# Two mixer layers with routed experts: other places for the gated pieces, the router's loads and the last norms

## The chip, the cores and the metric

The kernel runs on one core of a Trainium2 chip. The time is the device time of one execution in microseconds (us), the median of several runs. A separately profiled execution gives the trace. PE is the matmul engine (PEld its weight loads), DVE the vector engine, ACT the activation engine, POOL the general-purpose engine, SP the queue that only issues transfers. Each engine carries out its instructions in the order of the program.

## The reference

There are 16 sequences of 256 tokens, 128 wide, 4096 tokens in all. Each of two layers computes

```
xn = layernorm(x)
x  = x + mixer(xn) * silu(experts(xn))
```

- Layer 0 mixer: gated linear attention with 4 heads, keys of 128 and values of 32. `q`, `k`, `v`, a gate `g` and a decay `gk = log_sigmoid(xn Wgk1 Wgk2 + b) / 16` are projections. Within chunks the decayed product of `q` and `k` is masked to the lower triangle and weighs `v`, and a state carries over chunks; the result is normed per head, multiplied by `silu(g)` and projected by `Wo`.
- Layer 0 experts: softmax over 8 gates, the best two per token. An expert is `a * sigmoid(b)` with `a, b = split(xn W1[e] + b1[e])`, 256 each, then the common `Wo` and `bo`; the two are summed by weight.
- Layer 1 mixer: causal softmax attention with 16 heads of 8.
- Layer 1 experts: 16 experts, the best two, `tanh(xn mag) * cos(softplus(xn freq) + 0.1 + phase)` over 256 columns, then `down`; the weighted sum of the two is normed (RMS, weight `norm_w`).

## The kernel before

The tokens are eight blocks of 512 (`NB`), each four tiles of 128 (`NTL`). `xs` (the stream), `xnx` (normed, with two routing weights per token) and `xnTs` (normed, turned) stay on the chip. The mixer's result of a block is written over `xnTs` (`s_sbs`). Experts work on slots: each (token, choice) pair gets a place sorted by expert, 128 slots of one expert are a tile, 71 tiles in layer 0 and 79 in layer 1. The rows of a tile are fetched by an indirect DMA on POOL's queue (`slot_in`, line 378), and results are scattered back by another (`slot_out`, line 390).

The order on PE, DVE, ACT and SP is the order in which Python writes the instructions. Generators write them in pieces; each `yield` is a break at which another generator may write a piece.

- **Start.** `normed0` norms the eight blocks (`normed_T`, line 207: statistics and normalisation on DVE, turning on PE) and `route` (line 246) sorts the slots; at every second break `main` writes a piece. `main` is `gated()`: for each block `decays` (11 pieces: logarithms, running sums, scaled `q` and `k`) alternates with `mixed` of the block before (13 pieces: masked products `pA` copied by line 609, `v` weighed, norm, projection).
- **Layer-0 products.** `experts0` (line 677) goes over the tiles in 18 batches of `CP0 = 4`. Per tile: eight PE matmuls into one of two `pf` buffers (line 728), the sigmoid on ACT (lines 733 to 737), the gate on DVE (line 744, written one tile later). Per batch: the second product `pe` (line 758) and its weighing (lines 760 to 762). Its weights `wt0` come by SP into six buffers, with a small bias tile each. Every break calls `spread()`, which issues one waiting row fetch or result, and adds `1.0 / RATE` = 1.25 to what is due of `main`; each whole one due writes a gated piece and calls `spread()` again. Fetches and results stand behind the last instruction marked `passed`.
- **The passage.** `for _ in main: next(cstream)`: after each remaining gated piece, one round of `combined`. A round advances every live block by one stage, and starts one more block if its mixer is done. Stages of a block: fetch the two results (`gg`); sum, sigmoid; update of the stream and statistics; normalisation and turning; router scores (line 784).
- **Early layer 1.** What is left of `combined` runs with three pieces of attention per round (`fill(3)`), then `route` with one per break. Attention's pieces are `both` (scores in two forms, lines 928 and 961, whose maxima on DVE and exponentials on ACT follow), `queries`, `weighted` (line 1011, copied to `yt` by line 1016), `normed`, `turned`, `projected`, and five of `setup` per block (`qT` copied by line 889).
- **Layer-1 products.** After `route`, weights and rows of the first batch of `CPB = 8` tiles are asked for. `experts` (line 1108) has its own breaks, each with a piece of attention.
- **The tail.** The rest of attention, three pieces at a time, alternates with rounds of `finished` (line 1188): fetch of the results, sum, RMS norm, sigmoid, multiplication by the mixer's `s_sbs`, sum with the stream, output. A block enters when attention is done with it.

Of the kernel before, what the change touches and what calls it, by code (L numbers as in the profile page):

```python
# [10 lines left out]
F32 = mybir.dt.float32  # L11
# [28 lines left out]
RATE = 0.8  # L40
# [18 lines left out]
def two_layer_kernel(  # L59
# [147 lines left out]
    def normed_T(pool, ps, b):  # L207

        xb, xn = xs[b], xns[b]
        mv = pool.tile([P, NTL, 2], F32, tag="mv", name="mv", bufs=3)  # L210
        for t in range(NTL):
            st = pool.tile([P, 6], F32, tag="st", name="st", bufs=2)
            nc.vector.bn_stats(st, xb[:, t, :])
            nc.vector.bn_aggr(mv[:, t, :], st)
        rs = pool.tile([P, NTL], F32, tag="rs", name="rs", bufs=3)
        nc.scalar.activation(rs, mv[:, :, 1], AF.Ln, bias=eps5)
        nc.scalar.activation(rs, rs, AF.Exp, scale=-0.5)
        yield
        pt = ps[0].tile([P, NTL, P], F32, tag=ps[1], name="ptn")
        for t in range(NTL):  # L220
            nc.vector.tensor_scalar(  # L221
                xn[:, t, :], xb[:, t, :], mv[:, t, 0:1], rs[:, t : t + 1], ALU.subtract, ALU.mult
            )
            nc.tensor.transpose(pt[:, t, :], xn[:, t, :], ident)  # L224
        nc.scalar.copy(xnTs[b], pt.rearrange("p t k -> p (t k)"))
        yield
# [19 lines left out]
    def route(pool, ps, sc, ne, slt, lay, emap, rm, ptag, tkw):  # L246
# [87 lines left out]
        yield  # L334
# [3 lines left out]
        for c in range(2):  # L338
            for n0 in range(0, NT32, NH):
# [16 lines left out]
                yield  # L356

# [6 lines left out]
        yield  # L364
        tb = pool.tile([P, 2, slt], F32, tag="rt_tb", name="tb")
        nc.scalar.copy(tb, pT)
        row, tok = tb[:, 0, :], tb[:, 1, :]
        nc.vector.scalar_tensor_tensor(row, row, float(P), tok, ALU.mult, ALU.add)
        nc.vector.tensor_scalar(seconds[lay], row, 4096.0, None, ALU.is_ge)
        nc.vector.scalar_tensor_tensor(toks[lay], seconds[lay], -4096.0, row, ALU.mult, ALU.add)  # L370
# [106 lines left out]
    c_ps = []  # L477
    ccmb = ctx.enter_context(ExitStack())
    ET = mybir.EngineType
    with ExitStack() as cg:  # L480
# [118 lines left out]
        def mixed(b):  # L599
# [3 lines left out]
            for s in range(NSQ):  # L603
                for t in (2 * s, 2 * s + 1):
                    pA = ps.tile([P, GH, P], F32, tag="ps", name="pA")
                    for h in range(GH):
                        ts = slice(t * P, (t + 1) * P)
                        nc.tensor.matmul(pA[:, h, :], kk[:, h, ts], qg[:, h, ts], start=True, stop=True)  # L608
                    passed(nc.vector.copy_predicated(
                        a_bufs[t % 2], bc(upper.bitcast(I32).unsqueeze(1), [P, GH, P]), pA  # L610
                    ))
                    yield
                pf = ps.tile([P, GH, P], F32, tag="ps", name="pf0")
                for h in range(GH):
                    ts = slice((2 * s + 1) * P, (2 * s + 2) * P)
                    nc.tensor.matmul(pf[:, h, :], kg[:, h, s, :], qg[:, h, ts], start=True, stop=True)
                a_off = wk_.tile([P, GH, P], F32, tag="aoff", name="aoff")
# [59 lines left out]
        def experts0(hp, pe_):  # L677
# [3 lines left out]
            def loads(j0, n):  # L681
                wts, nbs = [], []
                for j in range(j0, j0 + n):
                    reg = tile_expert(emap0, j, E0)
                    wt = hp.tile([P, 2 * H0], F32, tag="wt0", name="wt0", bufs=6)
                    nc.sync.dma_start(wt, w1[:, bass.ds(reg, 1), :].rearrange("p e h -> p (e h)"))
                    nb = hp.tile([P, 4], F32, tag="nb0", name="nb0", bufs=8)
# [24 lines left out]
            for k, (j0, n) in enumerate(batches):  # L712
# [8 lines left out]
                for i in range(n):  # L721
# [5 lines left out]
                    for c in range(4):  # L727
                        nc.tensor.matmul(  # L728
                            pf[:, c, :], wts[i][:, c * P : (c + 1) * P], xgT[:, i, :], start=True, stop=True
                        )  # L730
                    sg = hp.tile([P, 2, P], F32, tag="sg0", name="sg0", bufs=3)
# [24 lines left out]
                for i in range(n):  # L756
                    for c in range(2):
                        nc.tensor.matmul(pe[:, i, :], gts[i][:, c, :], sb_wo0[:, c, :], start=(c == 0), stop=(c == 1))  # L758
                og = hp.tile([P, CP0, D], F32, tag="og0", name="og0")
# [7 lines left out]
        def combined(b):  # L767
# [13 lines left out]
            yield from normed_T(cmb, c_ps, b)  # L781
# [10 lines left out]
        with tc.manual_schedule(engines={ET.Activation, ET.PE, ET.DVE, ET.SP}):  # L792
# [25 lines left out]
            hp0.close()  # L818
            cmb = ccmb.enter_context(tc.tile_pool(name="cmb", bufs=2, side="left"))
            sc1 = cmb.tile([P, NT32, E1], F32, name="sc1", bufs=1)  # L820
            with tc.tile_pool(name="gpc", bufs=2, space=PSUM) as pc_:
                c_ps[:] = [pc_, "pc"]
                cstream = staged([combined(b) for b in range(NB)], lambda b: b in mixed_)
                for _ in main:
                    next(cstream, None)
# [4 lines left out]
    with ExitStack() as c1:  # L830
# [41 lines left out]
        def attention():  # L872
# [5 lines left out]
            def setup(b):  # L878
# [6 lines left out]
                def q_part(i):  # L885
# [3 lines left out]
                    passed(nc.vector.tensor_copy(qT[i], pq))  # L889
# [111 lines left out]
            def weighted(i):  # L1001
# [14 lines left out]
                later.append(lambda: passed(nc.vector.tensor_copy(yt, yx)))  # L1016
# [75 lines left out]
        def weights_of(j0, n):  # L1092

            wts = []
            for j in range(j0, j0 + n):
                reg = tile_expert(emap1, j, E1)
                wt = hp.tile([P, WROW], F32, tag="wt", name="wt", bufs=CPB + 1)
# [4 lines left out]
        def rows_of(j0, n):  # L1102

            xg = hp.tile([P, n, DX], F32, tag="xg", name="xg")
# [83 lines left out]
        def finished(b):  # L1188

            gg = results(hp, 1, b, "xg")  # L1190
# [17 lines left out]
            nc.vector.tensor_tensor(acc, acc, s_sbs[b], ALU.mult)  # L1208
            yield
            nc.vector.tensor_tensor(sq, sq, acc, ALU.mult)  # L1210
            nc.vector.tensor_tensor(sq, xs[b], sq, ALU.add)
            nc.sync.dma_start(ov[b], sq)
            yield

        wk_ = c1.enter_context(tc.tile_pool(name="l1wk", bufs=2, side="right"))
        pS = c1.enter_context(tc.tile_pool(name="l1pS", bufs=2, space=PSUM))
        ps = c1.enter_context(tc.tile_pool(name="l1ps", bufs=2, space=PSUM))
        pf_ = c1.enter_context(tc.tile_pool(name="l1pf", bufs=2, space=PSUM))
        pieces, ahead, later, done = attention(), [], [], set()
# [21 lines left out]
        with tc.manual_schedule(engines={ET.Activation, ET.PE, ET.DVE, ET.SP}):  # L1241
# [3 lines left out]
            for _ in cstream:  # L1245
                fill(3)
            with tc.tile_pool(name="rt1", bufs=1) as rt1:
                for _ in route(rt1, pf_, sc1, E1, SLT, 1, emap1, starts(rt1, E1), "pf", {"tag": "pf"}):
                    fill(1)
            ccmb.close()  # L1250
            hp = c1.enter_context(tc.tile_pool(name="l1h", bufs=2))
            batches = [(j0, min(CPB, SLT - j0)) for j0 in range(0, SLT, CPB)]
            got = weights_of(*batches[0]), rows_of(*batches[0])
# [10 lines left out]
            ends = staged([finished(b) for b in range(NB)], lambda b: b in done)  # L1264
            while fill(3):
                next(ends, None)
            for _ in ends:
                pass
# [53 lines left out]
```

## Time and profile before

| | before |
|---|---|
| runs, median (lowest to highest) | 1162.42 us (1159.44 to 1168.86), 3 runs |
| profiled execution | 1160.43 us, span 1158.7 us |
| busy in the span | PE 878.0 (76%), DVE 763.6 (66%), ACT 588.5 (51%), POOL 394.3 (34%) |
| mean granted PE clock | 0.863 |
| layer-0 products, 115 to 420 us | PE busy 252.07 |
| passage, 425 to 531 us | PE busy 62.67, DVE 61.75 |
| early layer 1, 531 to 643 us | DVE busy 90.40 |
| hand-over, 643 to 660 us | PE busy 8.52 |
| layer-1 products, 660 to 1054 us | PE busy 341.13 |
| tail, 1054 to 1158.7 us | PE busy 68.45 |

The profiled time is that of the whole execution; the span runs from its first to its last instruction. Busy times are sums over an engine's instructions, and a matmul's includes the granted clock: the same matmul takes longer at a lower clock.

### The profile page before, as it was taken

Reading aid. Unit: us, or ns where it says so; the run is one execution under the profiler, and the core shown is the slowest. Engines: PE = TensorE matmul, PEld = TensorE weight load, DVE = VectorE, ACT = ScalarE, POOL = GpSimd, SP = SyncE. Lnnn points to the kernel's source line nnn. Section 1 sums busy time; section 2 is a strip of 40 time slices with the busy share of each in tenths; the row PEclk is TensorE's granted clock in tenths of the full one; section 3 lists DMA queues with packets and bytes.
Section 4 is the critical chain, followed back from the end, with each engine's and each line's share of the span. In section 5 each row is a group of like instructions: output and inputs, shape, how many; then the busy total and the mean of one; then the engine's idle time right before and its main releaser. Section 6 shows DMA issues by size and latency. Waiting matters only on the chain.

```text
span 1158.7 us, 17715 instructions
## 1 busy us (share of the span) xinstructions
PE 878.0 (76%) x6394; PEld 623.3 (54%) x6394; DVE 763.6 (66%) x1442; ACT 588.5 (51%) x1059; POOL 394.3 (34%) x422
## 2 busy tenths in 40 slices
PE   6554887888879854867666688887789899788782
PEld 4323666666657633543334366665576666565451
DVE  5777555665565748544689388767678777785843
ACT  3314576866666735432113265656465666565543
POOL 2000545463535320000111426534554664433110
PEclk9977899998889985677679699999899899998666
DMA  4040497532323222000040413431442243212311
GB/s 121 1 74 11 127 227 152 132 109 79 110 78 91 69 71 73 19 1 1 0 74 1 151 44 112 138 128 29 136 139 77 89 144 128 59 63 71 92 37 36
DMA packets 88415, 95.41 MB, mean 82 GB/s; under 512 B 22228, under 2 KB 64040, under 8 KB 88328
## 3 DMA queue, kind: packets, MB, share of 16 engines
q1 hardware_dynamic: 78632, 74.32, 23.4%
q0 software_dynamic: 9696, 19.97, 6.7%
q8 instruction: 50, 0.82, 0.3%
q14 instruction: 37, 0.30, 0.1%
HBM read 78.03 MB, written 22.51 MB: 87 GB/s over the span
## 4 chain that ended last, share of the span: by engine, by line
PE 43%; DVE 29%; ACT 14%; issue 7%; DMA 4%; POOL 1%; SPq 1%; DVEq 0%; POOLq 0%; ACTq 0%
PE pq L547 5%; PE pf L728 4%; PE Sq L928 3%; PE pe L1178 3%; PE pm L1153 3%; PE pe L758 3%; DVE negm L940 2%; PE Sk L961 2%; DVE vt L1139 2%; PE yx L1011 2%; PE pA L608 2%; DVE vt L1143 2%; DVE z L1135 1%; PE Sq L922 1%; DVE mx L938 1%
## 5 line engine op out<-in xcount | busy, mean ns | idle before, releaser
L390 POOL DMA_INDIRECT yd<-og,row x150 | 157.5, 1050 | 201.1 <-DVE og L762 102.3
L378 POOL DMA_INDIRECT xg<-xnd,tok x150 | 150.9, 1006 | 105.3 <-PE pz L511 52.9
L971 POOL TENSOR_SCALAR_AFFINE_SELECT pr<-pr 128x1024 f32<-128x1024 f32 x64 | 70.8, 1108 | 262.5 <-ACT pr L968 262.3
L968 ACT ACTIVATE pr<-Sk 128x1024 f32<-128x1024 f32 x96 | 98.0, 1021 | 108.0 <-PE Sk L961 107.7
L961 PE MATMUL Sk<-qm,kT 32*128 32x256 f32 x768 | 125.1, 449 | 24.9 <-DVE negm L940 17.3
L928 PE MATMUL Sq<-km,qT 32*128 32x256 f32 x768 | 129.1, 455 | 16.1 <-DVE mx L938 7.8
L728 PE MATMUL pf<-xgT,wt 128*128 128x128 f32 x568 | 84.2, 298 | 28.6 <-issue 12.1
L928 PEld LDWEIGHTS Sq<-km,qT 32*128 32x128 f32 x768 | 70.6, 208 | 63.0 <-issue 34.7
L728 PEld LDWEIGHTS pf<-xgT,wt 128*128 128x128 f32 x568 | 77.4, 209 | 43.4 <-issue 23.5
L961 PEld LDWEIGHTS Sk<-qm,kT 32*128 32x128 f32 x768 | 74.3, 209 | 38.9 <-DVE negm L940 23.2
L940 DVE TENSOR_REDUCE negm<-Sq 128x8 f32<-128x1024 f32 x64 | 78.1, 1220 | 23.5 <-PE Sq L928 14.1
L733 ACT ACTIVATE sg<-pf,nb 128x128 f32<-128x128 f32 x142 | 44.3, 364 | 67.0 <-PE pf L728 66.6
L744 DVE SCALAR_TENSOR_TENSOR gt<-pf,nb,sg 128x128 f32<-128x128 f32 x142 | 42.7, 344 | 40.6 <-ACT sg L737 34.6
L922 PE MATMUL Sq<-mq,identb 128*128 128x512 bf16 x128 | 42.4, 416 | 18.1 <-DVE mx L938 9.5
L1178 PE MATMUL pe<-wt,th 128*128 128x128 f32 x316 | 41.9, 288 | 16.4 <-DVE th L1170 16.3
L1178 PEld LDWEIGHTS pe<-wt,th 128*128 128x128 f32 x316 | 38.8, 199 | 23.9 <-DVE th L1170 12.7
L224 PE MATMUL ptn<-ident,xnx 128*128 128x128 f32 x64 | 18.6, 438 | 41.6 <-DVE xnx L221 41.6
L938 DVE TENSOR_REDUCE mx<-Sq 128x8 f32<-128x1024 f32 x32 | 39.0, 1218 | 15.0 <-PE Sq L928 8.9
L758 PE MATMUL pe<-sb_wo,gt 128*128 128x128 f32 x284 | 41.4, 302 | 8.9 <-DVE gt L744 4.9
L347 ACT ACTIVATE ohj<-hi,place 128x568 bf16<-128x568 bf16 (+1 forms) x16 | 12.8, 798 | 68.2 <-DVE hi L346 65.1
L758 PEld LDWEIGHTS pe<-sb_wo,gt 128*128 128x128 f32 x284 | 38.6, 212 | 15.7 <-DVE gt L744 5.9
L1016 DVE COPY yt<-yx 128x512 f32<-128x512 f32 x32 | 21.9, 686 | 33.8 <-PE yx L1011 33.7
(269 smaller groups left out, 2089.5 us busy)
## 6 DMA issues: line engine op xcount, KB each, us to landing
wt<-bank SPq DMA_DIRECT2D x79, 385.0 KB
wt<-in_w_dram SPq DMA_DIRECT2D x71, 256.0 KB
gg<-yd SPq DMA_DIRECT2D x32, 256.0 KB
xnd<-xnx SPq DMA_DIRECT2D x16, 260.0 KB
xg<-xnd,tok POOLq DMA_INDIRECT x150, 3.1
yd<-og,row POOLq DMA_INDIRECT x150, 2.3
x<-in_x_dram SPq DMA_DIRECT2D x8, 256.0 KB
bank<-in_freq_dram SPq DMA_DIRECT2D x1, 2048.0 KB
```

The costliest lines, as they stand in the source:

```text
L378: return nc.gpsimd.indirect_dma_start(out=xg[:, i, :], out_offset=None, in_=xnds[lay], in_offset=bass.IndirectOffsetOnAxis(ap=toks[lay][:, ...
L390: give = nc.gpsimd.indirect_dma_start(out=yds[lay], out_offset=bass.IndirectOffsetOnAxis(ap=rows[lay][:, j : j + 1], axis=0), in_=og[:, i, ...
L547: nc.tensor.matmul(pq[:, c], w_[:, h * DK : (h + 1) * DK], xnT, start=True, stop=True)
L728: nc.tensor.matmul(pf[:, c, :], wts[i][:, c * P : (c + 1) * P], xgT[:, i, :], start=True, stop=True)
L758: nc.tensor.matmul(pe[:, i, :], gts[i][:, c, :], sb_wo0[:, c, :], start=(c == 0), stop=(c == 1))
L922: nc.tensor.matmul(S[:, c], identb, mq, start=True, stop=False, skip_group_check=True)
L928: nc.tensor.matmul(S[:, c, js, :], qT[part][r, tq], km[r, js, tk], start=not diag, stop=True, skip_group_check=True,)
L940: passed(nc.vector.tensor_reduce(ng, S, AX.X, ALU.max, negate=True))
L961: nc.tensor.matmul(S[:, c, js, :], kT[part][r, tk], qm[r, js, :], start=True, stop=True, skip_group_check=True,)
L968: nc.scalar.activation(pr, S, AF.Exp, scale=scale)
L971: pooled(nc.gpsimd.affine_select(pr_, pr_, pattern=[[0, 8], [1, P]], compare_op=ALU.is_ge, fill=0.0, base=0, channel_multiplier=-1,))
L1178: nc.tensor.matmul(pe[:, i - i0, :], ths[i // 2][:, 2 * (i % 2) + c, :], wts[i][:, 2 * H1 + c * D : 2 * H1 + (c + 1) * D], start=(c == 0), ...
```

## The change

1. In `experts0` a break (`yield`) is added between the product `pf` and its sigmoid, and between `pe` and its weighing. `RATE` goes from 0.8 to 1.33, since there are now 11 breaks per batch of four instead of 6.
2. In `mixed` the break after `pA` stands ahead of the masked copy instead of behind it, and a break is added between `pf0` and its copy: 15 pieces instead of 13.
3. `wt0` has eight buffers instead of six, `nb0` nine instead of eight.
4. The passage writes four gated pieces per round of `combined` instead of one.
5. In `combined`, the normalisation runs on ACT instead of DVE (a DVE instruction for the bias is added).
6. Until layer 1's `route` is over (`early`), the copies to `qT` and `yt` run on ACT instead of DVE.
7. `route` makes `tok` ahead of the arithmetic for `row`. In layer 1 it tells its caller when the experts of the tiles and when the tokens are known; at the first the first batch's weights are asked for, at the second its rows, the first four at once. For that, `wt` and `xg` move into a pool of their own (`hx`), `sc1` too (`psc1`), and the pool of `combined` is closed before `route`.
8. `finished` is cut in two: `weighed` (up to the product of the sigmoid and the normed sum, kept in `xns`) runs for all blocks from the end of the products on; `finished` multiplies by `s_sbs`, adds the stream and writes, once attention is done with the block.

```diff
-RATE = 0.8
+RATE = 1.33
...
+        if on_act:
+            nb = pool.tile([P, NTL], F32, tag="nb", name="nb", bufs=3)
+            nc.vector.scalar_tensor_tensor(nb, mv[:, :, 0], -1.0, rs, ALU.mult, ALU.mult)
         yield
...
+                nc.scalar.activation(
+                    xn[:, t, :], xb[:, t, :], AF.Identity, scale=rs[:, t : t + 1], bias=nb[:, t : t + 1]
+                )
...
-        yield
+        yield "experts"
...
+        tb = pool.tile([P, 2, slt], F32, tag="rt_tb", name="tb")
+        nc.scalar.copy(tb, pT)
+        row, tok = tb[:, 0, :], tb[:, 1, :]
+        nc.vector.scalar_tensor_tensor(row, row, float(P), tok, ALU.mult, ALU.add)
+        nc.vector.tensor_scalar(seconds[lay], row, 4096.0, None, ALU.is_ge)
+        nc.vector.scalar_tensor_tensor(toks[lay], seconds[lay], -4096.0, row, ALU.mult, ALU.add)
+        yield "tokens"
...
+                    yield
                     passed(nc.vector.copy_predicated(
                         a_bufs[t % 2], bc(upper.bitcast(I32).unsqueeze(1), [P, GH, P]), pA
                     ))
-                    yield
...
+                yield
                 a_off = wk_.tile([P, GH, P], F32, tag="aoff", name="aoff")
...
-                    wt = hp.tile([P, 2 * H0], F32, tag="wt0", name="wt0", bufs=6)
+                    wt = hp.tile([P, 2 * H0], F32, tag="wt0", name="wt0", bufs=8)
...
+                    yield
                     sg = hp.tile([P, 2, P], F32, tag="sg0", name="sg0", bufs=3)
...
+                yield
                 og = hp.tile([P, CP0, D], F32, tag="og0", name="og0")
...
-            yield from normed_T(cmb, c_ps, b)
+            yield from normed_T(cmb, c_ps, b, True)
...
-                for _ in main:
-                    next(cstream, None)
+                for _ in cstream:
+                    for _ in range(3):
+                        next(main, None)
+                    if next(main, main) is main:
+                        break
...
-                    passed(nc.vector.tensor_copy(qT[i], pq))
+                    if early:
+                        nc.scalar.copy(qT[i], pq)
+                    else:
+                        passed(nc.vector.tensor_copy(qT[i], pq))
...
-                later.append(lambda: passed(nc.vector.tensor_copy(yt, yx)))
+                later.append(lambda: nc.scalar.copy(yt, yx) if early else passed(nc.vector.tensor_copy(yt, yx)))
...
-            nc.vector.tensor_tensor(acc, acc, s_sbs[b], ALU.mult)
-            yield
-            nc.vector.tensor_tensor(sq, sq, acc, ALU.mult)
-            nc.vector.tensor_tensor(sq, xs[b], sq, ALU.add)
-            nc.sync.dma_start(ov[b], sq)
-            yield
+            yield
+            nc.vector.tensor_tensor(xns[b], sq, acc, ALU.mult)
+            ready.add(b)
+            yield
+
+        def finished(b):
+            o = hp.tile([P, NTL, D], F32, tag="z", name="o1", bufs=2)
+            nc.vector.tensor_tensor(o, xns[b], s_sbs[b], ALU.mult)
+            nc.vector.tensor_tensor(o, xs[b], o, ALU.add)
+            nc.sync.dma_start(ov[b], o)
...
+            ccmb.close()
+            batches = [(j0, min(CPB, SLT - j0)) for j0 in range(0, SLT, CPB)]
...
+                    if step == "experts":
+
+                        got = weights_of(*batches[0])
+                    if step == "tokens":
+                        got = got, rows_of(*batches[0])
+                        fetch(4)
                     fill(1)
...
-            ends = staged([finished(b) for b in range(NB)], lambda b: b in done)
-            while fill(3):
+            ends, b = staged([weighed(b) for b in range(NB)]), 0
+            while b < NB:
+                fill(3)
                 next(ends, None)
-            for _ in ends:
-                pass
+                while b in done and b in ready:
+                    finished(b)
+                    b += 1
```

## The prediction

> **What bounds the kernel now.** I read the page first, then busy time by stage, cut where the work changes: layer-0 products with gated pieces (115 to 420 us), the passage (425 to 531), early layer 1 with its router (531 to 643), the hand-over (643 to 660), the layer-1 products (660 to 1054), the tail. Columns: stretch, length, busy us of PE, PEld, DVE, ACT, POOL with counts, granted clock, DMA share, GB/s.
>
> ```profile
> 115.00:420.00 305.00, 252.07 (x1733) 197.60 (x1733) 175.58 (x316) 201.32 (x427) 146.32 (x139) 0.91 0.45 113
> 425.00:531.00 106.00, 62.67 (x331) 45.92 (x329) 61.75 (x147) 41.63 (x73) 0.65 (x2) 0.69 0.14 40
> 531.00:643.00 112.00, 78.44 (x495) 44.09 (x497) 90.40 (x154) 23.54 (x32) 13.85 (x20) 0.74 0.12 20
> 643.00:660.00 17.00, 8.52 (x53) 4.40 (x48) 2.11 (x3) 1.61 (x2) 10.64 (x11) 0.62 0.76 249
> 660.00:1054.00 394.00, 341.13 (x3064) 248.55 (x3066) 294.92 (x510) 234.72 (x335) 195.34 (x190) 0.97 0.31 96
> 1054.00:1158.70 104.70, 68.45 (x484) 40.46 (x476) 57.15 (x114) 48.62 (x126) 14.14 (x13) 0.69 0.21 62
> ```
>
> No engine bounds the whole. PE bounds the two product stages (83% and 87%). In the passage and the tail nobody is over 66%: these are chains from engine to engine. Early layer 1 is DVE's (81%). In the hand-over nearly everything stands still.
>
> The waits of the layer-0 stage (160 to 400 us) say who stands there: engine, line, whom it waits for, total us, times, longest.
>
> ```profile
> ACT sg L733 <- PE pf L728: 46.8, 30, 5.2
> DVE gt L744 <- ACT sg L737: 32.2, 19, 3.3
> DVE og L760 <- PE pe L758: 14.1, 10, 4.2
> DVE a L609 <- PE pA L608: 11.2, 9, 2.1
> PE pf L728 <- issue: 12.1, 4, 4.6
> PE pf L728 <- ACT sg L736: 6.8, 2, 3.4
> ```
>
> The first four are a reader queued directly behind its own product. The last two are what it costs PE: two buffers of pf, released by the gate, and a gate that comes late.
>
> The chain of waits through the passage: start, us, what.
>
> ```profile
> 426.25 3.70 DMA gg<-yd
> ...
> 437.59 1.11 DVE xnx L221 x4
> 438.70 0.61 DVE sl L779
> 439.33 0.70 DVE x L780
> ...
> 477.61 1.89 PE plg L784 x8
> ```
>
> From 430 to 472 it is almost only DVE doing `combined`, with one gated piece per round.
>
> Timeline of the hand-over and of the end: start, us, instruction, in brackets the idle time before it.
>
> ```profile
> 651.96 0.45 PE L1115 MATMUL pxt<-ident,xg 128*128 128x128 f32 x1 [5.98 <-issue]
> 659.80 0.69 DVE L1016 COPY yt<-yx 128x512 f32<-128x512 f32 x1 [13.09 <-PE yx L1011]
> ```
>
> ```profile
> 1144.15 0.59 ACT L1052 COPY xnT<-p_s 128x512 f32<-128x512 f32 x1 [1.25 <-PE p_s L1051]
> 1148.07 0.69 DVE L1193 TENSOR_TENSOR acc<-gg 128x512 f32<-128x512 f32 x1 [4.68 <-DMA gg<-yd]
> 1155.32 0.38 SPq L1212 DMA_DIRECT2D out_dram<-sq  x1
> ```
>
> Attention's last block is complete at 1144.74, and the output leaves at 1155.32: in between only block 7's fetch and norm run, alone.
>
> **The change, part by part.** The profiled execution took 1160.43 us (span 1158.70), 2.0 under the median of 1162.42.
>
> **Layer-0 products.** Before: 109 breaks x 1.25 = 136 gated pieces, of 24 per block. Now two more breaks per product (one per tile, one per batch): 198 x 1/1.33 = 148 pieces, of 26 per block. With the 17 pieces run earlier that leaves 192-153 = 39 before and 208-165 = 43 now, the same place in the work, so no work changes stage. What changes is the order. Gain: reader and product no longer stand back to back; the copy of pA likewise. Upper end: layer 1 already breaks between product and reader, and its PE is busy 341.13 of 394 at clock 0.97. Layer 0 at that rate: 252.07 x 0.91/0.97 = 236.5, over 0.866 = 273, that is 32 less. Loss: a gate (0.61 a pair) was queued on DVE ahead of the pieces of its break; now it follows the piece in the first break and only the second break stands between it and the next pf product, empty one time in four. Of 26 pieces eight hold DVE: four `scaled` 1.23, two `sums` 1.23+2.30+0.18+0.69 = 4.4, kg 1.4, sg 2.6 with its wait: mean 2.2, plus the gate 0.6, less some 0.6 of PE work in the second break = 2.2 per case, in 71 tiles x 0.75 x 8/26 = 16.4 cases: 36 more, if none of today's stalls goes. Eight weight buffers instead of six ask for a tile two tiles (2 x 300/71 = 8 us) earlier; at 161.55 the chain shows a 12.79 us landing behind a bank copy, and PE idles 4.33 before the product at 178.53, so up to 4 is to be had. SP issues as many DMAs as before, earlier; POOL gets more turns; it now waits 93.4 us for og in this stage, so it can take them. Behind a gate that waits stand, on DVE, the next piece's operations and og, and for those PE's pq and POOL's results wait: that is rival 1. Between -32 and +36 I take **-10**: the nearest row is layer 1's, same shape and same two banks, but PE already stands at 83%; a third of its advantage.
>
> **Passage.** Before, eight rounds with a piece each fill 426 to 477, then some 31 pieces take 54 us, 1.74 each. Now four pieces follow each round: 11 rounds for 43 pieces. The pieces' work is that of 39 old ones: 39 x 1.74 = 68. A round costs DVE 0.69+0.69+0.69+0.70 for acc, acc, sl, x, 1.75 for the eight statistics, 0.2 for sc, 0.2 for the new nb = 4.9 per block; 6.8 blocks fall here: 33. All hidden in the pieces' gaps: 68, -38. None: 101, -5. DVE is busy 25 of the pieces' 68, so I take half: 84.5, -21.5. The last round of block 6 moves into layer 1: +3. **-18**. The four normalisations per block go from DVE (1.11) to ACT; nearest row L733, two in 0.63, so 1.26, within an ACT that is busy 41.63 of 106.
>
> The Trainium skill, "ScalarE: Activation LUTs", section "What ACT_TABLE_LOAD costs", speaks against that move: an activation with pointer operands for scale and bias pays a fixed cost for each, which for 128 columns makes by estimate 0.39 each, 1.64 for four. By it ACT would carry 2.6 us more over the passage than by the row, and the time below would be at most 1115 instead of 1112; no row of this trace has both pointers.
>
> **Early layer 1.** Six rounds at three pieces and 25 router breaks take 43 attention pieces, which holds 5 qT and 4 yt copies at 0.684, now on ACT, plus block 7's normalisation, 1.1-0.2: 7.1 off a DVE that is busy 81%: 5.7. On ACT (23.54 of 112 busy) they queue behind exponentials of 1.0, and their readers on PE wait for that: 0 to 1 per copy, half lost at worst. Bounds -7, +3; **-5**. The router's tiles now lie where `combined` had its own and wait for block 7's last readers; DVE and ACT pass those anyway before they reach the router, and only POOL's memset is held, needed first at 579.47: nothing.
>
> **Hand-over.** The eight weight tiles (9 DMAs, 7.08 us of issuing on SP) now go out after the expert map at 595, their 3 MB beside xnd's; on SP nothing but the eight xnd writes stands ahead of them. They leave the window where DMA moves 249 GB/s. Four rows are asked for as soon as the tokens exist, ahead of 5 us of router arithmetic on DVE, instead of after it. Before: first row issue 646.5, first transpose 651.96, the second four at 659.66. Now: tokens near 640, four issues of 1.27 to 645.6, the rest to 650, landing in 3.6 (the row at 117.95): second transposes at 653.6. **-6**; bounds -10 (all hidden by the two fills) and -3 (POOL held by the last DVE instruction it is put behind).
>
> **Tail.** `weighed` no longer waits for attention. From s at 1144.74 remain two DVE operations of 0.69, then the same 3.4 from the DMA issue to the end: 1149.5 instead of 1158.7, -9.2. Block 6's norm also stands on attention's own chain, ahead of pr at 1133.13 (2.5) and ahead of y at 1141.54 (1.7); both go earlier. Two blocks' DVE work (2 x 2.5) moves to the front of the tail, where DVE is half idle: +2.5. **-11**; bounds -14, -4.
>
> Sum: -10-18-5-6-11 = -50: 1110.4 against the profiled 1160.4, and with the 2.0 to the median **1112**.
>
> **Rivals.**
> 1. *The late gate rules layer 0* (slower). Place: L744 behind the piece's DVE operation, PE at L728 waiting. The other parts give -40, so slower than now by 1% takes +52 here, 0.73 us per tile over 71 tiles; +55 gives 1177. For: DVE is at 57% with long scans (2.30). Against: bound +36, and layer 1 does the same at 87%.
> 2. *The passage stays a chain*: pieces and rounds queue behind each other on DVE and ACT, -5 there, and the products gain nothing: 1112+13+10 = 1135. For: 1.74 per piece at clock 0.69 already is latency. Against: DVE idles 44 us of 106.
> 3. *Layer 0 reaches layer 1's rate*: -32 instead of -10: 1090. For: 46.8+32.2 of reader waits. Against: those engines are not the bound.
> 4. *Nothing is won in sum*, within 1%: products +20 and the passage -5 together, 1112+30+13 = 1155.
>
> **How the numbers follow.** Forecast (1100 to 1124) 0.45, rival 3 0.20, rival 2 0.22, rival 4 0.06, rival 1 0.07. Two bounds that dominate, 34 each way and 17 each way, add as squares to 38: 1074 to 1150, which holds rivals 2 and 3 and leaves 4 and 1 out. A measurement of this kernel can tell about 1% (its three runs span 0.8%). Faster 0.87, same 0.06, slower 0.07.
>
> **What the profile after will show.** Right: the stage of layer-0 products some 10 shorter with L733's wait for pf well under 46.8 and the clock not lower; gg to first attention product in 85 to 90, clock above 0.69; no DVE gap like 13.09 before the first layer-1 product; last output DMA within 3 us of attention's last copy, no L1193 behind it. Wrong: L728 waiting for L744 in many tiles, total over 36; a passage above 100; first row landing as late as now after the tokens.

## The result, and the profile after

| | before | changed |
|---|---|---|
| median (lowest to highest), 20 runs each | 1162.34 us (1158.24 to 1173.06) | 1169.70 us (1162.04 to 1174.91) |
| ratio to before | | 1.0048, 95% interval 1.0025 to 1.0072 |
| profiled span | 1158.7 us | 1166.5 us |
| mean granted clock | 0.863 | 0.852 |

The change makes the kernel half a per cent slower. The forecast was 1112, faster by 4%, with 1074 to 1150 as its range: wrong in sign and outside the range.

Divided at the same events in both profiles (first product of layer 0, first fetch of results for `combined`, first `pk` of layer 1, first product of layer 1, last second product of layer 1), the time goes like this. "Again" are second profiles of the same two kernels, taken on one chip (runs before_again and after_again).

| stage, us | before | again | changed | again | forecast | got, by the two "again" |
|---|---|---|---|---|---|---|
| start | 123.5 | 124.0 | 122.6 | 122.6 | 0 | -1.4 |
| layer-0 products | 301.6 | 304.0 | 338.6 | 338.5 | -10 | **+34.5** |
| passage | 107.2 | 107.6 | 103.7 | 103.6 | -18 | -4.0 |
| early layer 1 and hand-over | 127.8 | 132.1 | 120.7 | 120.7 | -11 | -11.4 |
| layer-1 products | 388.1 | 388.6 | 391.9 | 391.9 | 0 | +3.3 |
| tail | 110.5 | 110.1 | 89.0 | 91.4 | -11 | -18.7 |

One stage takes back what the others give. Busy time by stage (stretch, length, PE, PEld, DVE, ACT, POOL, granted clock, DMA share, GB/s), first the layer-0 products of before, then the changed kernel:

```profile
123.50:425.10 301.60, 252.64 (x1721) 198.68 (x1718) 172.22 (x313) 197.83 (x423) 142.56 (x136) 0.91 0.44 109
```

```profile
122.60:461.20 338.60, 264.73 (x1761) 205.49 (x1759) 176.05 (x317) 203.13 (x430) 140.22 (x134) 0.90 0.39 96
461.20:565.00 103.80, 58.58 (x311) 40.06 (x311) 56.46 (x137) 50.48 (x97) 1.44 (x3) 0.67 0.14 41
565.00:685.60 120.60, 81.95 (x569) 46.68 (x569) 88.90 (x142) 34.15 (x50) 26.07 (x31) 0.78 0.22 52
...
1077.50:1166.50 89.00, 63.43 (x515) 38.75 (x513) 59.17 (x116) 47.99 (x127) 19.88 (x18) 0.79 0.26 76
```

In the layer-0 products DVE (176.05) and ACT (203.13) have within 3% the work they had, and the clock is 0.90 against 0.91. PE is 12 us busier and idle for 74 us instead of 49. So this stage is not short of an engine: two thirds of what it lost are waits of PE. Directly ahead of the product, PE's idle time grew from 28.6 to 43.1 us (the number behind the last bar of each row, first before, then changed):

```profile
L728 PE MATMUL pf<-xgT,wt 128*128 128x128 f32 x568 | 84.2, 298 | 28.6 <-issue 12.1
```

```profile
L738 PE MATMUL pf<-xgT,wt 128*128 128x128 f32 x568 | 87.0, 303 | 43.1 <-issue 18.8
```

Who waits, in the changed kernel from 160 to 456 us (engine, line, for whom, total, times, longest; L738 is the product, L744 to L748 the sigmoid, L755 the gate, L628 the copy of pf0):

```profile
ACT sg L744 <- PE pf L738: 53.5, 26, 7.1
DVE gt L755 <- ACT sg L748: 48.6, 21, 8.3
PE pf L738 <- issue: 18.3, 6, 6.4
PE pf L738 <- ACT aoff L628: 9.4, 3, 6.2
```

The break was put between product and reader so that the readers would not wait. The rows of before in the prediction (46.8 and 32.2) are of a shorter window; over the whole stage the sigmoid's wait falls from 66.6 to 61.7 and the gate's rises from 34.6 to 48.8. Why PE waits shows in the timeline (start, us, instruction, in brackets the idle time before it):

```profile
232.60 0.63 ACT L744 ACTIVATE sg<-pf,nb 128x128 f32<-128x128 f32 x2 [0.34 <-PE pf L738]
...
233.54 2.29 DVE L531 TENSOR_TENSOR_SCAN cum<-rmask,sp 128x1024 f32<-128x1024 f32 x1
233.70 0.42 ACT L748 ACTIVATE sg<-sg 128x256 f32<-128x256 f32 x1
...
236.07 0.69 DVE L537 TENSOR_TENSOR cum<-cum,mid 128x512 f32<-128x512 f32 x1
236.69 0.72 DVE L619 COPY_PREDICATED a<-upper,pA 128x512 f32<-128x512 int32 x1
...
237.31 0.59 DVE L755 SCALAR_TENSOR_TENSOR gt<-pf,nb,sg 128x128 f32<-128x128 f32 x2
...
238.00 2.05 PE L738 MATMUL pf<-xgT,wt 128*128 128x128 f32 x8 [2.59 <-ACT sp L523]
```

The sigmoid is complete at 234.12, and from then on nothing but its place in DVE's queue keeps the gate: the scan, its correction and a masked copy of the piece go first, 3.2 us. The next product needs the bank that this gate frees, and PE stands 2.59 us. The profile puts this wait down to an activation, not to the gate; in the waits of PE the gate does not appear for the product at all. Yet all 18 waits of over 0.3 us that PE has ahead of this product end 0.10 us after the end of a gate, and all 12 of them in before end 0.05 to 0.10 us after one. So the gate ends these waits, whichever instruction the profile names.

The tail did better than forecast. The last output leaves 2.07 us after attention's last copy begins, and no norm stands in between:

```profile
1160.99 0.58 ACT L1071 COPY xnT<-p_s 128x512 f32<-128x512 f32 x1 [1.25 <-PE p_s L1070]
1161.61 0.69 DVE L1234 TENSOR_TENSOR o<-xnx,xnT 128x512 f32<-128x512 f32 x1 [2.87 <-ACT xnT L1071]
1162.34 0.69 DVE L1235 TENSOR_TENSOR o<-x,o 128x512 f32<-128x512 f32 x1
1163.06 0.37 SPq L1236 DMA_DIRECT2D out_dram<-o  x1
```

At the hand-over, PE's first transposition of rows comes 1.21 after the work before it, not 5.98:

```profile
676.41 0.33 PE L1134 MATMUL pxt<-ident,xg 128*128 128x128 f32 x1 [1.21 <-DMA xg<-xnd,tok]
```

### The profile page after: what moved, and what is told of

Same layout as the page of the kernel before. It is cut to its first block, busy times and chain, and to the rows that moved or that the text cites. A ratio compares the mean times of both kernels' runs of the same rounds, so it can differ in the third digit from the quotient of the medians.

```text
span 1166.5 us, 17683 instructions
## 1 busy us (share of the span) xinstructions
PE 868.3 (74%) x6394; PEld 617.0 (53%) x6394; DVE 752.2 (64%) x1410; ACT 602.6 (52%) x1099; POOL 395.0 (34%) x422
## 4 chain that ended last, share of the span: by engine, by line
PE 43%; DVE 29%; ACT 16%; issue 6%; DMA 3%; POOL 2%; SPq 1%; DVEq 0%; POOLq 0%; ACTq 0%
PE pq L556 5%; PE Sq L947 4%; PE pf L738 4%; PE pm L1172 3%; PE pe L1197 3%; DVE negm L959 3%; PE Sk L980 2%; PE pe L769 2%; DVE vt L1158 2%; PE Sq L941 2%; PE pf L1145 2%; PE yx L1030 2%; PE pz L520 1%; DVE ohp L350 1%; DVE vt L1162 1%
## 5 line engine op out<-in xcount | busy, mean ns | idle before, releaser
L398 POOL DMA_INDIRECT yd<-og,row x150 | 152.3, 1015 | 249.4 <-DVE og L774 131.5
L386 POOL DMA_INDIRECT xg<-xnd,tok x150 | 154.6, 1031 | 107.2 <-DVE row L379 52.3
L947 PE MATMUL Sq<-km,qT 32*128 32x256 f32 x768 | 127.8, 451 | 17.3 <-DVE mx L957 8.0
L738 PE MATMUL pf<-xgT,wt 128*128 128x128 f32 x568 | 87.0, 303 | 43.1 <-issue 18.8
L738 PEld LDWEIGHTS pf<-xgT,wt 128*128 128x128 f32 x568 | 79.8, 214 | 62.0 <-issue 32.3
L744 ACT ACTIVATE sg<-pf,nb 128x128 f32<-128x128 f32 x142 | 44.0, 361 | 61.7 <-PE pf L738 61.7
L755 DVE SCALAR_TENSOR_TENSOR gt<-pf,nb,sg 128x128 f32<-128x128 f32 x142 | 42.3, 343 | 50.0 <-ACT sg L748 48.8
L529 DVE SCALAR_TENSOR_TENSOR sp<-pz,sp 128x1024 f32<-128x1024 f32 x16 | 19.5, 1219 | 45.5 <-ACT sp L524 45.5
L1145 PEld LDWEIGHTS pf<-xgT,wt 128*128 128x128 f32 x316 | 41.0, 200 | 8.3 <-issue 8.2
```

The lines of the kernel that those rows point to most:

```text
L386: return nc.gpsimd.indirect_dma_start(out=xg[:, i, :], out_offset=None, in_=xnds[lay], in_offset=bass.IndirectOffsetOnAxis(ap=toks[lay][:, ...
L398: give = nc.gpsimd.indirect_dma_start(out=yds[lay], out_offset=bass.IndirectOffsetOnAxis(ap=rows[lay][:, j : j + 1], axis=0), in_=og[:, i, ...
L738: nc.tensor.matmul(pf[:, c, :], wts[i][:, c * P : (c + 1) * P], xgT[:, i, :], start=True, stop=True)
L947: nc.tensor.matmul(S[:, c, js, :], qT[part][r, tq], km[r, js, tk], start=not diag, stop=True, skip_group_check=True,)
L1145: nc.tensor.matmul(pf[:, k, :], wts[i][:, c * P : (c + 1) * P], xgTs[i // 4][:, i % 4, :], start=True, stop=True)
```

## The experiments

"Products" and "passage" are lengths of the stages of the table above. Ratios are to before on the same chip. Stage lengths come from one profile each and are compared across chips; on the chips used, that of the first four runs apart, the medians of before agree within 0.1% (1163.31 to 1164.42). The edits of parts 1 and 2 look like this, and the runs put them in or leave them out:

```diff
+                    yield            # break per tile, between pf and its sigmoid
                     sg = hp.tile([P, 2, P], F32, tag="sg0", name="sg0", bufs=3)
...
+                yield                # break per batch, between pe and its weighing
                 og = hp.tile([P, CP0, D], F32, tag="og0", name="og0")
```

**The changed kernel with one part taken out: four runs that did not settle it.** p_old leaves out both breaks, p_no_tile_break the one per tile, p_old_mixed part 2. p_gate_ahead keeps all and moves the gate:

```diff
+                    for f in pend:   # the gate of the tile before
+                        f()
                     yield
                     sg = hp.tile([P, 2, P], F32, tag="sg0", name="sg0", bufs=3)
...
-                    for f in pend:
-                        f()
```

> The changed kernel with the two new breaks of the layer-0 products taken out again (6 breaks per batch; RATE 0.736, so that the same 148 gated pieces are written by the end of the stage). Everything else of the change stays. Theory A (the new breaks themselves cost the 35 us, because they let a piece's ACT and DVE work in ahead of the readers, and the two pf banks stay taken): the first fetch of results comes near 426 us instead of 461.65, and the total near 1170-35 = 1135. Theory B (the finer pieces of `mixed`, 26 per block, or the earlier weights cost it): it stays near 460, total near 1168.

> The changed kernel with one thing moved: the gate of the tile before is written ahead of the first break, directly behind the product pf, instead of behind the piece and the sigmoid. Theory A1 (of the two readers it is the gate, queued on DVE behind the piece, that holds the bank, as rival 1 had it): most of the 35 us come back, first fetch near 430 to 440, total near 1140 to 1148. Theory A2 (it is the sigmoid, queued on ACT behind the piece's logarithms, that makes gate and bank late; the gate's own place matters little): the fetch stays at 450 to 465, total 1158 to 1172.

> The changed kernel without the break between pf and its sigmoid; the break between the second product and its weighing stays (7 breaks per batch, RATE 0.855, again 148 pieces). Theory A: the break per tile carries the loss (71 of them against 18), so fetch near 426 to 432, total near 1135 to 1142. If the loss is in the break per batch, or in B, the fetch stays above 450.

> The changed kernel with the breaks of `mixed` as before (copy of pA directly behind its product, no break behind pf0: 13 pieces, 24 per block; RATE 1.453, so that 136 pieces are written by the end of the products). Theory B: 15 to 35 us less, fetch at 427 to 447. Theory A: the copies wait for pA again, 0 to 8 us more, total 1168 to 1178.

These ran on another chip, on which the kernel before took 1231.40 us. Ratios to before: 0.9833 (0.9783 to 0.9883), 0.9883 (0.9838 to 0.9928), 0.9863 (0.9794 to 0.9932), 0.9894 (0.9843 to 0.9944); products 344.6, 357.8, 347.6, 350.6. The expectations named absolute times of a faster chip, and neither before nor the changed kernel was profiled there, so these runs settle none of the theories. The products are shortest with both breaks out; the ratios' intervals overlap. One thing can be read: PE's idle time ahead of the product is 51.9 us in p_old_mixed, where the gate stands behind the piece, and 27.8 in p_gate_ahead, where it does not (the two differ in part 2 as well; p_old has 23.5). Yet p_gate_ahead has the longest products of the four. What moving the gate would give in the whole changed kernel is therefore not shown.

**Before and changed on one chip, the breaks alone, and the change without the products' parts.** only_breaks is the kernel before with part 1 alone; no_products is the changed kernel without parts 1 to 3.

> The kernel before, unchanged, for a profile on the chip that runs the next three. All theories: products (first layer-0 product to first fetch of results) near 302 us, as in its first profile; if this chip is a slower one, more, and then the others have to be read against this profile and not against the first.

> The changed kernel, unchanged, on the same chip. All theories: 1.005 of before; products 37 us longer than in the profile of before, tail 21 shorter, early layer 1 7 shorter. If the products are as long in both here, the 37 us of the first two profiles belong to the chip and not to the change.

> The kernel before with the two new breaks of the layer-0 products alone (RATE 1.453, so that 136 pieces of the old kind are written as before). Theory A (the breaks cost the 35 us): 30 to 40 slower, ratio 1.025 to 1.035, in the products stage alone. Theory B (pieces of `mixed`, weights): within 8 of before.

> The changed kernel with parts 1 to 3 taken out (breaks of the products, breaks of `mixed`, weight buffers; RATE 0.8 again): passage, early layer 1, hand-over and tail as changed. Theory A and B alike: the products as before, and what the other parts gave stays: 23+7+3 less than before, ratio 0.970 to 0.978. If the gains of the tail and early layer 1 are only time moved out of the products, it is 0.99 to 1.0.

| run | median, us | ratio to before | products | passage | tail |
|---|---|---|---|---|---|
| before_again | 1168.11 (one run) | | 304.0 | 107.6 | 110.1 |
| after_again | 1168.77 | 1.0039 (1.0017 to 1.0061) | 338.5 | 103.6 | 91.4 |
| only_breaks | 1184.68 | 1.0186 (1.0130 to 1.0242) | 326.1 | 106.9 | 110.3 |
| no_products | **1129.44** | **0.9707 (0.9651 to 0.9763)** | 305.8 | 100.1 | 88.7 |

The stage is shown: without parts 1 to 3 the products are as before, and the gains of the other parts stay. By its ratio to before that is the fastest version of all runs. The breaks alone cost 22.1 of the 34.5, less than theory A had (30 to 40).

**Which reader: gate or sigmoid?** Four forms of only_breaks. ob_gate_ahead moves the gate as in the diff above; only the sigmoid is left behind the piece. ob_sig_ahead moves the break behind the sigmoid; only the gate is left. ob_double keeps the number of breaks and pieces, but both stand behind all readers. ob_tile_only drops the break per batch.

```diff
 # ob_sig_ahead: the first break of the tile
-                    yield
                     sg = hp.tile([P, 2, P], F32, tag="sg0", name="sg0", bufs=3)
...
                     gt = hp.tile([P, 2, P], F32, tag="gt0", name="gt0", bufs=6)
+                    yield
                     for f in pend:
                         f()
```

> The kernel before with the two breaks (the run only_breaks: ratio 1.0186, products 326.1 us against 304.0), and the gate of the tile before written ahead of the first break, directly behind the product: only the sigmoid is left behind the piece. Theory A1 (the gate behind the piece holds the bank): products 304 to 312, ratio 1.000 to 1.007. Theory A2 (the sigmoid behind the piece's ACT work is what comes late): products 320 to 330, ratio 1.013 to 1.022. Theory C (neither; the finer spread of the pieces costs it): 320 to 330 too.

> As only_breaks, but the first break stands behind the sigmoid: product, sigmoid, break, gate of the tile before, break. Only the gate is left behind the piece. Theory A1: products 320 to 330, ratio 1.013 to 1.022. Theory A2: 304 to 312, ratio 1.000 to 1.007. Theory C: 320 to 330.

> As only_breaks with the same number of breaks and the same RATE, but both breaks of a tile stand behind product, sigmoid and gate, as the single one did before; the break between second product and weighing stays. Theories A1 and A2 (a reader behind a piece): products 302 to 312, ratio 0.998 to 1.007. Theory C (spread of the pieces, or the break per batch): 318 to 330, ratio 1.011 to 1.022.

> As only_breaks without the break between second product and weighing (10 breaks per batch, RATE 1.321): the break between product and sigmoid alone. Theories A1 and A2: products 320 to 328, ratio 1.013 to 1.021. If the break per batch carries the loss: 302 to 310, ratio 0.998 to 1.006.

| run | ratio to before | products | PE idle ahead of the product |
|---|---|---|---|
| before_again | | 304.0 | 27.8 |
| only_breaks | 1.0186 (1.0130 to 1.0242) | 326.1 | 45.2 |
| ob_gate_ahead | 1.0057 (1.0026 to 1.0088) | 308.7 | 29.3 |
| ob_sig_ahead | 1.0159 (1.0088 to 1.0230) | 325.3 | 44.8 |
| ob_double | 1.0004 (0.9970 to 1.0038) | 301.7 | 29.7 |
| ob_tile_only | 1.0251 (1.0178 to 1.0325) | 331.4 | 42.9 |

It is the gate (theory A1). Written ahead of the piece, it takes back 17.4 of 22.1, although the sigmoid still stands behind the piece; with the sigmoid ahead and the gate behind, 0.8. As many breaks in another place cost nothing, so it is not the finer spread. The break per batch is innocent (the break per tile without it is even 5 longer, past what was expected, with no more idle time ahead of the product). The last column shows the mechanism: PE's idle time there goes up with the gate behind the piece and comes back with the gate ahead of it. The page rows, only_breaks first, then ob_gate_ahead:

```profile
L728 PE MATMUL pf<-xgT,wt 128*128 128x128 f32 x568 | 87.0, 304 | 45.2 <-issue 17.1
```

```profile
L728 PE MATMUL pf<-xgT,wt 128*128 128x128 f32 x568 | 80.6, 289 | 29.3 <-ACT sg L739 11.2
```

The profile names "issue" (no releaser found) and several activations for these waits. But all 19 of over 0.3 us in only_breaks, and all 12 in ob_gate_ahead, end 0.10 us after the end of a gate. One of only_breaks that is put down to ACT's copy of the turned rows (L703), with the last two operations of a piece and the gate on DVE ahead of it:

```profile
334.16 0.68 DVE L647 TENSOR_TENSOR yT<-po,sq 128x512 f32<-128x512 f32 x1
334.87 0.69 DVE L648 TENSOR_TENSOR yT<-yT,sg 128x512 f32<-128x512 f32 x1
335.48 1.12 DVE L745 SCALAR_TENSOR_TENSOR gt<-pf,nb,sg 128x128 f32<-128x128 f32 x4
336.18 1.19 PE L728 MATMUL pf<-xgT,wt 128*128 128x128 f32 x4 [4.82 <-ACT xgT L703]
```

(The row of the gate holds four instructions, two tiles; the first tile's gate ends near 336.1.) What is left in ob_gate_ahead, 29.3, is what before has too.

**The rest of the loss.**

```diff
 # mixed_only: part 2, in the kernel before
+                    yield
                     passed(nc.vector.copy_predicated(
                         a_bufs[t % 2], bc(upper.bitcast(I32).unsqueeze(1), [P, GH, P]), pA
                     ))
-                    yield
...
+                yield
                 a_off = wk_.tile([P, GH, P], F32, tag="aoff", name="aoff")
```

weights_only is part 3 in the kernel before; breaks_mixed is parts 1 and 2.

> The kernel before with part 2 alone: the copy of pA one break later and a break behind pf0 (15 pieces, 26 per block; RATE 0.736, so that 148 are written by the end of the products). If the finer pieces carry the rest of the loss: products 312 to 318 against 302 to 304. If they only take waits away from DVE (line 609 waits 11 to 18 us for pA now): 298 to 305.

> The kernel before with part 3 alone: eight weight buffers instead of six, nine for the bias. If earlier loads help behind the bank copies, as the prediction had it: products 298 to 302. If they carry the rest of the loss (more transfers at once, the row fetches and bias tiles late): 310 to 316. If neither: 302 to 305.

> The kernel before with parts 1 and 2 together, without the weight buffers (RATE 1.33, 148 pieces). Parts alone: breaks 326.1 us (+22), pieces of `mixed` 305.8 (+2). Theory X (the two together: the pieces' copies and the copy of pf0 now stand on DVE and ACT at the head of the next piece, ahead of the late readers): products 334 to 342, ratio 1.026 to 1.034. Theory Y (they add up, and the rest is the weights in company with the breaks): 325 to 331, ratio 1.018 to 1.023.

| run | ratio to before | products | PE idle ahead of the product |
|---|---|---|---|
| mixed_only | 0.9992 (0.9974 to 1.0011) | 305.8 | 22.5 |
| weights_only | 0.9995 (0.9967 to 1.0022) | 301.4 | 28.6 |
| breaks_mixed | 1.0265 (1.0214 to 1.0316) | 338.7 | 43.9 |

Alone, part 2 costs 1.8 and part 3 gives 2.6, both near what two profiles of the same kernel differ by (302 and 304). Parts 1 and 2 together give 338.7, the whole loss, as theory X had it in size: 34.7, of which 22.1 + 1.8 are the parts' own and 10.8 come from their company.

Theory X's reason for these 10.8 was that the copies of part 2 now stand at the head of the next piece, ahead of the late readers (L619 in the timeline above is such a copy). That would show as more idle time of PE, and it hardly does: ahead of the product it is 43.9, against 45.2 in only_breaks. The stage's rows, only_breaks first, then breaks_mixed:

```profile
124.40:450.50 326.10, 256.12 (x1743) 201.18 (x1742) 175.68 (x317) 202.31 (x428) 143.75 (x134) 0.91 0.38 100
```

```profile
122.50:461.20 338.70, 266.67 (x1749) 206.85 (x1747) 176.19 (x317) 202.79 (x429) 140.05 (x134) 0.87 0.39 97
```

Of the 12.6 us between them, 10.6 are busy time of PE, at a granted clock of 0.87 against 0.91, and 2 are idle time. The changed kernel, whose stage is as long, has 264.73 busy at 0.90. Why PE is busy longer with both parts together was not tried; the cause of these 10.8 stays open.

**The passage and the tail.** Three forms of no_products: np_pass1 writes one piece per round again, np_dve normalises on DVE again, np_old_tail has the old `finished`.

```diff
 # np_pass1
-                for _ in cstream:
-                    for _ in range(3):
-                        next(main, None)
-                    if next(main, main) is main:
-                        break
+                for _ in main:
+                    next(cstream, None)
 # np_dve
-            yield from normed_T(cmb, c_ps, b, True)
+            yield from normed_T(cmb, c_ps, b)
```

> The changed kernel without parts 1 to 3 (the run no_products: ratio 0.9707, passage 100.1 us), and the passage with one piece per round again, as before. Theory P1 (the passage is one chain through DVE and ACT, whichever way pieces and rounds are mixed, and the 7 us come from the normalisation on ACT): passage 98 to 102, ratio 0.968 to 0.974. Theory P2 (four pieces per round give the 7 us): passage 106 to 110, ratio 0.974 to 0.980.

> The changed kernel without parts 1 to 3 (no_products: ratio 0.9707, passage 100.1 us, early layer 1 116.9), and the normalisation of `combined` on DVE again. Theory N1 (ACT is the worse place, as np_pass1 with 113.9 against 107.2 suggests: the four normalisations stand behind the sigmoids and logarithms of ACT's queue and PE's turning waits): passage 92 to 96, ratio 0.963 to 0.968; this is then the best version. Theory N2 (with four pieces per round the wait is hidden, and DVE is relieved): passage 100 to 104, ratio 0.970 to 0.976.

> The changed kernel without parts 1 to 3 (no_products: tail 88.7 us against 110), and with the old `finished`, which waits for attention. Theory T1 (the early norms give all of it): tail 108 to 112, ratio 0.988 to 0.992. Theory T2 (11 from the norms, the rest because attention was three pieces further when the products ended): tail 99 to 102, ratio 0.979 to 0.984.

| run | ratio to before | passage | early layer 1 | tail |
|---|---|---|---|---|
| no_products | 0.9707 (0.9651 to 0.9763) | 100.1 | 116.9 | 88.7 |
| np_pass1 | 0.9884 (0.9841 to 0.9927) | 113.9 | 117.3 | 92.4 |
| np_dve | 0.9772 (0.9725 to 0.9818) | 103.4 | 122.3 | 93.0 |
| np_old_tail | 0.9840 (0.9803 to 0.9877) | 100.5 | 119.6 | 104.1 |

The two parts of the passage need each other. With one piece per round, the normalisation on ACT costs 6.3 (113.9 against 107.6): the activations stand behind sigmoids and logarithms, and PE's turning waits. With four per round it gives 3.3 there and 5.4 in early layer 1. The 5.4 is little more than the 4.3 by which two profiles of before differ in early layer 1. Four per round give 13.8 with it and 4.2 without. P1 and N1 are wrong; P2 and N2 hold, P2 by more than it said. PE's wait for the normalisation, one piece per round (430 to 550 us), then four (432 to 533 us):

```profile
PE ptn L232 <- ACT xnx L225: 35.9, 7, 12.8
```

```profile
PE ptn L232 <- ACT xnx L225: 15.2, 4, 9.4
```

In the tail the early norms give 15.4 against no_products, and 6.0 come without them (104.1 against 110.1): between T1 and T2. The same tail took 88.7 to 93.0 in five profiles (the changed kernel twice, no_products, np_pass1, np_dve), so the 15.4 may be as little as 11. Attention that is further when the products end can explain the 6.0; this was not tried apart.

## Why the prediction was wrong

- **Layer-0 products, -10: the step that failed.** The stage came out 34.5 longer. The mechanism and its place were in the text: the gate queued on DVE behind the piece of the first break, a bank not freed, PE waiting at the product. The choice between the bounds, -32 and +36, failed. It went by "the nearest row is layer 1's, same shape and same two banks", at a third of that stage's advantage; but in before PE has 0.0 us of idle time ahead of layer 1's first product (the row below), so that stage said nothing of what a late gate costs in layer 0. ob_gate_ahead, ob_sig_ahead and ob_double show what it costs: 17.4 of the 22.1 us that the breaks add hang on the place of one DVE instruction. That rival 1's bound of 36 lies so near the 34.5 is luck: it reckoned 16.4 cases of 2.2 for the breaks, which alone took 22.1, and 10.8 more came from the company of part 2, which the working had not priced as a loss and whose cause is open. Its count of "eight" pieces of 26 that hold DVE also left out five: the four copies of pA and the piece with yT.

```profile
L1126 PE MATMUL pf<-xgT,wt 128*128 128x128 f32 x316 | 43.5, 280 | 0.0
```

- **The gain side was empty.** The forecast reckoned with readers that no longer wait. Over the whole stage the sigmoid waits 4.9 less and the gate 14.2 more; ACT and DVE were not the bound of the stage, as the text against rival 3 said itself.
- **Eight weight buffers** were to give up to 4, from a wait of 4.33 us before the product at 178.53. That wait was misread: the weights had landed at 174.34 by the chain's row, and the wait ends 0.1 us after the end of a gate. weights_only still has it, 4.33 again, and its products took 301.4 against 302 and 304. The rows of before:

```profile
177.81 0.61 DVE L744 SCALAR_TENSOR_TENSOR gt<-pf,nb,sg 128x128 f32<-128x128 f32 x2 [3.29 <-ACT sg L737]
178.53 0.77 PE L728 MATMUL pf<-xgT,wt 128*128 128x128 f32 x2 [4.33 <-ACT sg L733]
```

- **Passage, -18: the hidden half was not hidden.** 68 for the pieces plus 33 for the rounds, nothing hidden, is 101; measured 103.6, and 100.1 in no_products. As a sum the bound of -5 was right (no run takes its two terms apart), "I take half" was not, and rival 2 had the reason. In the changed kernel's chain of waits the round's and the pieces' operations follow one another without overlap (start, us, what):

```profile
470.86 1.24 DVE sp L529
472.12 2.30 DVE cum L531
474.45 0.18 DVE mid L536
474.65 0.69 DVE cum L537
475.34 0.63 DVE a L619
475.98 0.58 DVE sl L791
476.58 0.70 DVE x L792
```

  Sums of a piece, then a masked copy, then the round's update: DVE is 54% busy in this stage (56.46 of 103.80), and still it is what most of this stretch waits for.
- **The normalisation on ACT** was taken as hidden at 1.26 per block. The prediction set against it the Trainium skill, "ScalarE: Activation LUTs", section "What ACT_TABLE_LOAD costs", by whose fixed costs for pointer operands four should take 1.64 by estimate. The trace of the changed kernel agrees with the page and not with the row that was used: four take 1.63 to 1.65.

```profile
544.01 1.65 ACT L225 ACTIVATE xnx<-x,nb,rs 128x128 f32<-128x128 f32 x4
```

  The same four activations cost 6.3 in one order of the queue and gave 3.3 in the other, so the place in the queue decided.
- **Early layer 1 and hand-over, -11:** -11.4 by the pair of profiles on one chip. Right in size; two profiles of before differ by 4.3 here, so no single term of it is confirmed, and the agreement may be luck.
- **Tail, -11:** mechanism right, size too small: -18.7, of which 11 to 15.4 are the norms. The end chain was sized right (9.2 forecast, 9.0 measured: the span now ends 4.9 us after attention's last copy is complete, where before it ended 13.96 after). The other 9.7 stand against a forecast of 4.2 less 2.5; 6.0 of the tail's gain come without the norms, which the sum did not have, and no run says from what.
- **The sum.** Without the first item the forecast's own terms make 1122; no_products is 1129.44. The range was too narrow because the two ends of the products' term, uneven about its -10, were joined with the others as if they were independent and even. The low chance given to rival 1 (0.07) rested on one row of another stage. The layer-1 products, put at 0, came out 3.3 longer; runs in which nothing bears on that stage lie between 387 and 391.

## What to carry to other kernels

A break between a product and its readers moves the readers back in their own engines' queues, behind whatever the break lets in. The reader whose end frees the buffer should be written ahead of the break: that brought back 17.4 of 22.1 us here, and the other reader, left behind it, kept at most the remaining 4.7. Two buffers and engines that work in the order of the program turn a late release into a wait of the producer, and the profile can name another instruction for it than the releaser. Whether a suspected instruction is the releaser can be read from the trace: here every wait ended 0.05 to 0.10 us after a gate. When a bundle of edits comes out even, measure by stage first: here one stage lost what three others had won, and leaving its parts out gave 3%.

## What the runs showed of the hardware

The kernel before took 1231.40 us on one chip and 1162 to 1164 us in the medians elsewhere. The first experiments' profiles there have the usual granted clock (0.851 to 0.868 in the mean), but both product stages are long: layer 1's took 420.5 in p_old, against 387 to 392 elsewhere. In these four profiles DVE stands idle for over 0.5 us, without a releaser that the profile can name, 9 to 14 times, 14 to 42 us in all; in every other profile that happens at most once. What stops it there was not found; no reference was profiled there.

In all waits of over 0.3 us ahead of a layer-0 product, in before, only_breaks, ob_gate_ahead and the changed kernel, PE started 0.05 to 0.10 us after the end of a gate on DVE, which had read the bank.
